# Top-32 attention on one core: the selection on quarters instead of halves of the scores

## The chip, the cores and the metric

The kernel runs on one core of a Trainium2 chip. The metric is the device time of one execution in microseconds (us). Three executions of the kernel before took 1880.09, 1892.16 and 1891.26 us; their median is 1891.26. A core has five engines that run at the same time, each through its own queue in order: TensorE (PE in the profile; PEld is its weight load), VectorE (DVE), ScalarE (ACT), GpSimd (POOL) and SyncE (SP, here for transfers). They wait for one another through semaphores.

## The reference

For each of 8 batches: 512 text rows `x` (256 wide) attend to 1024 context rows `cx` (192 wide) with 4 heads of 32. Of each row of 1024 scores only the 32 largest count; the softmax is over these. The mean over the heads weights the context; what comes out modulates a long convolution, an MLP and two layer norms, and then a mixture of 8 experts (one expert for each row, and a shared one).

```python
scores = einsum('bthd,bghd->bhtg', Q, K) / sqrt(DH)
topv, topi = top_k(scores, 32)
probs = softmax(topv, axis=-1)
attn = zeros_like(scores).at[bi, hi, ti, topi].set(probs)
attn_mean = attn.mean(axis=1)
...
x = x + tanh(g_xattn) * xattn(layernorm(x), ctx, ...)
x = x + tanh(g_ffn) * moe(layernorm(x), ...)
```

The masks are all true in these inputs.

## The kernel before

**Stages.** Batch by batch there are four streams of work: `prepare` (layer norm of `x`, keys `kT`, queries `qT`), `attention`, `mixed` with `after_mix` (convolution by a transform, modulation, MLP, shared expert), and `routed` (blocks of 128 rows for one expert each, whose results are added into `out` by indirect transfers that GpSimd issues). While batch b is in attention, batch b-1 is in `mixed` and `after_mix` (`behind`, L1378), batch b+1 in `prepare`, and the routed blocks of earlier batches lie between. After the last attention there is a tail of the last batch's `mixed`, `after_mix` and routed blocks.

**The order.** Nothing is issued directly. The class `Plan` (L50) notes every operation with an assumed duration (`time`, L137), its predecessors and its buffers. `order` (L220) then lays out all engines' queues by taking, among the operations that can begin first, the one noted earliest; `issue` (L318) issues them in that order. This is why nearly every instruction has line L326 in the profile. Where the plan finds TensorE idle, `busy` (L1407) puts in filler matmuls, `idle<-ones` at L1409, whose result nobody reads. A change of one operation therefore moves others on every engine.

**The attention step.** There are 64 steps: 8 batches, 4 tiles of 128 rows, 2 pairs of heads (L913). In each, for the two heads i of the pair:

- `scores` (L893), one step ahead: TensorE multiplies `qT` and `kT` into two PSUM banks, ScalarE copies these to `sc`, 128 rows by 1024 scores.
- The selection (L935 to L969). VectorE's `max` (MAX8 in the profile) returns the 8 largest of each row, `match_replace` overwrites these 8 so that the next `max` finds the next 8. Searching 1024 columns is avoided: score g and score g+512 form a pair. VectorE writes the higher of each pair to the first half of `mn` (L943), GpSimd the lower one to the second half, as integer sum less the higher one on the bits of the floats (L945, L946), so that no bit is lost. Four rounds of `max` and three of `match_replace` give the 32 largest of the 512 higher ones, with `left` as the working copy (L948 to L956); one `max` gives the 8 largest of the lower ones (L965). The 8th of the merged last eight and these eight is the 32nd largest score, `th` (L966 to L969), unless more than 8 of the 32 are lower ones.
- The weights. ScalarE computes exp into `e`; VectorE multiplies it by `score >= th` and sums it (L977, SCALAR_TENSOR_TENSOR); ScalarE counts by signs how many scores reach `th` (L979, `cnt`) and divides by the sum; GpSimd adds the heads into `acc` (L984). After both pairs `weighted` (L875) transposes `acc` and multiplies it with the context.

`mn`, `left`, `e`, `top` have two buffers each, `sc` four. At the end the kernel tests that every row had exactly 32 scores from `th` upward and that all masks are true (L1415 to L1424). If not, a general path computes everything again under `tc.If` (L1425).

Of the kernel before, what the change touches and what calls it, by code (L numbers as in the profile page):

```python
# [12 lines left out]
F32 = mybir.dt.float32  # L13
# [3 lines left out]
I32 = mybir.dt.int32  # L17
AF = mybir.ActivationFunctionType
ALU = mybir.AluOpType
# [3 lines left out]
P = 128  # L23
# [326 lines left out]
def tile_kernel(ctx: ExitStack, tc: tile.TileContext, a: dict, out: bass.AP):  # L350
# [3 lines left out]
    G, DV = cx.shape[1:]  # L354
    H, DH = 4, 32
    KTOP = 32
    HID = a["L0_xattn_W1"].shape[1]
    NST = a["L0_xattn_A_re"].shape[1]
    NE, _, NI = a["L0_ffn_rt_gate"].shape
# [4 lines left out]

    L = T // 2
    NL, NFFT = L // P, 2 * L
    SCALE = 1.0 / float(np.sqrt(np.float32(DH)))


# [15 lines left out]
    pk = ctx.enter_context(tc.tile_pool(name="pk", bufs=2))  # L385
# [10 lines left out]
    V, S, GP, TE, SY = (plan.engine(n, e) for n, e in (  # L396
        ("DVE", nc.vector), ("ACT", nc.scalar), ("POOL", nc.gpsimd), ("PE", nc.tensor), ("SP", nc.sync)))
# [495 lines left out]
    def scores(b, s, t, h0):  # L893

        plan.lead += LEAD_S
        n = f"{b}_{t}_{h0}"
        sc = [pq.tile([P, G], F32, tag="s", name=f"sc{n}_{i}") for i in range(2)]
        for q in range(G // 512):
            qs = slice(q * 512, (q + 1) * 512)
            pS = []  # L900
            for i in range(2):
                hp = slice((h0 + i) * DH, (h0 + i + 1) * DH)
                pS.append(ps_sc.tile([P, 512], F32, tag="sc", name=f"pS{n}_{i}_{q}", bufs=2))
                TE.matmul(pS[i], s.qT[hp, t * P : (t + 1) * P], s.kT[hp, qs], start=True, stop=True)
            for i in range(2):
                S.copy(sc[i][:, qs], pS[i])
        plan.lead -= LEAD_S
        return sc

    def attention(states):  # L910


        steps = [(b, t, h0) for b in range(B) for t in range(NT) for h0 in range(0, H, 2)]  # L913
        ahead = scores(0, states[0], 0, 0)
        behind = None
        for k, (b, t, h0) in enumerate(steps):
            s, sc = states[b], ahead
            if k + 1 < len(steps):
                b_, t_, h_ = steps[k + 1]
                for _ in states[b_].prep:  # L920
                    pass
                ahead = scores(b_, states[b_], t_, h_)
            if (t, h0) == (0, 0):


                s.uT = pk.tile([DK + 1, 2, T], F32, tag="uT", name=f"uT{b}")
                GP.memset(s.uT[DK : DK + 1, 0, :], 1.0)
            if h0 == 0:
                acc = pk.tile([P, G], F32, tag="acc", name=f"acc{b}_{t}")
            n = f"{b}_{t}_{h0}"  # L930

            top = pk.tile([P, 2, KTOP + 8], F32, tag="top", name="top" + n)  # L935
            sm = pk.tile([P, 5, 2], F32, tag="sm", name="sm" + n)
            nm, nb, na, su, ri = (sm[:, k_, :] for k_ in range(5))
            e_, mn = [], []
            for i in range(2):
                m_ = pk.tile([P, 2, G // 2], F32, tag="mn", name=f"mn{n}_{i}")  # L940
                mn.append(m_)
                lo, hi = sc[i][:, : G // 2], sc[i][:, G // 2 :]
                V.tensor_tensor(m_[:, 0], lo, hi, ALU.max)  # L943
                mi = m_.bitcast(I32)
                GP.tensor_tensor(mi[:, 1], lo.bitcast(I32), hi.bitcast(I32), ALU.add)  # L945
                GP.tensor_tensor(mi[:, 1], mi[:, 1], mi[:, 0], ALU.subtract)  # L946
            for i in range(2):
                for r in range(KTOP // 8):  # L948
                    t8 = top[:, i, r * 8 : r * 8 + 8]
                    src = mn[i][:, 0] if r == 0 else left  # L950
                    V.max(t8, src)
                    if r == 0:
                        S.activation(nm[:, i : i + 1], t8[:, 0:1], AF.Copy, scale=-SCALE)
                        left = pk.tile([P, G // 2], F32, tag="left", name=f"left{n}_{i}")
                    if r < KTOP // 8 - 1:
                        V.match_replace(left, t8, src, TAKEN)  # L956
                e_.append(pk.tile([P, G], F32, tag="e", name=f"e{n}_{i}"))
                S.activation(e_[i], sc[i], AF.Exp, bias=nm[:, i : i + 1], scale=SCALE)
                if i == 0:
                    yield  # L960
                    if behind is not None:
                        behind()
                        behind = None
            for i in range(2):
                V.max(top[:, i, KTOP:], mn[i][:, 1])  # L965
            t8 = pk.tile([P, 2, 8], F32, tag="t8", name="t8" + n)  # L966
            for i in range(2):
                V.max(t8[:, i, :], top[:, i, KTOP - 8 :])
            th = t8[:, :, 7]  # L969

            S.activation(na, th, AF.Abs, scale=EPS32)
            for i in range(2):
                S.activation(nb[:, i : i + 1], th[:, i : i + 1], AF.Identity, bias=na[:, i : i + 1],
                             scale=-1.0)
            for i in range(2):
                c = (b * NT + t) * H + h0 + i
                V.scalar_tensor_tensor(e_[i], sc[i], th[:, i : i + 1], e_[i], ALU.is_ge, ALU.mult,  # L977
                                       accum_out=su[:, i : i + 1])
                S.activation(junk, sc[i], AF.Sign, bias=nb[:, i : i + 1], accum_out=cnt[:, c : c + 1])  # L979
            V.reciprocal(ri, su)  # L980
            for i in range(2):
                S.activation(acc if h0 + i == 0 else e_[i], e_[i], AF.Copy, scale=ri[:, i : i + 1])
                if h0 + i:
                    GP.tensor_add(acc, acc, e_[i])  # L984
            if h0 + 2 == H:
                behind = partial(weighted, b, s, t, acc)
            yield
        behind()

    def attention_masked(b, s):  # L990
# [3 lines left out]
        for t in range(NT):  # L994
            acc = pk.tile([P, G], F32, tag="acc", name=f"acc{b}_{t}")
            for h in range(H):
# [14 lines left out]
                for r in range(KTOP // 8):  # L1011
                    src = sc if r == 0 else wk_
                    V.max(top[:, r * 8 : r * 8 + 8], src)
                    if r == 0:
                        GP.tensor_scalar(sm[:, 0:1], top[:, 0:1], -SCALE, None, ALU.mult)
                    V.match_replace(wk_, top[:, r * 8 : r * 8 + 8], src, TAKEN)

                S.activation(top, top, AF.Exp, bias=sm[:, 0:1], scale=SCALE, accum_out=sm[:, 1:2])
                S.activation(sc, sc, AF.Exp, bias=sm[:, 0:1], scale=SCALE)
                S.activation(wk_, wk_, AF.Exp, bias=sm[:, 0:1], scale=SCALE)  # L1020
                GP.tensor_sub(sc, sc, wk_)
# [353 lines left out]
    for _ in states[0].prep:  # L1375
        pass
    att = plan.ahead(attention(states), LEAD_A)
    def behind(b):  # L1378

        s_, between, n = mixed(b, states[b]), (), n_mix + n_mlp  # L1380
        rows = None
        if b - 1 in TAKE:
            k = TAKE[b - 1]
            if b == B - 1:
                rows = [rows_of(blk[b - 1], i, f"{b - 1}_{i}", "xb" if i < 2 else "left")
                        for i in range(k)]
            k0 = max(0, k - BETWEEN)
            if k0:
                s_ = beside((s_, n_mix), (routed(b - 1, 0, k0, rows), k0))
            between = routed(b - 1, k0, k, rows)  # L1390
            n += k
        return chain([s_, after_mix(b, states[b], between)]), n
# [96 lines left out]
```

## Time and profile before

| | |
|---|---|
| median of three executions | 1891.26 us |
| the profiled execution | 1877.53 us |
| its span, first to last instruction | 1875.8 us |
| TensorE's granted clock, mean | 0.955 |
| VectorE busy | 1465.7 us, 78% of the span |
| GpSimd busy | 1089.6 us, 58% |
| ScalarE busy | 1173.7 us, 63% |
| TensorE busy, 380.7 us of it fillers | 1712.8 us, 91% |
| first and last start of a write to `mn` | 34.5 and 1596.0 us |

The page's group rows read: line, engine, operation, output `<-` inputs by their names in the program, shapes, number of instructions; then busy time in us and mean duration in ns; then the idle time of that engine just before such instructions, and what ended it. The rows by tile give the least, the median and the greatest duration in ns. A window's row has its start and end, its length, and the busy time (and number of instructions) of each engine, then TensorE's clock and the share and rate of the transfers. An engine's busy time includes time in which an instruction has begun but is held up inside the engine. The profiled execution is one run; its time stands below the three others.

### The profile page before, as it was taken

The page shows a single profiled execution, that of the slowest core. Times are in us where ns is not written, and L with a number is a line of the kernel's source. Part 1 is how long each engine was busy: PE and PEld are TensorE (multiplying, and loading weights), DVE is VectorE, ACT ScalarE, POOL GpSimd, SP SyncE. Part 2 cuts the span into 40 slices and gives each one's busy share as a digit, 9 for nine tenths or more (in the row PEclk, how much of TensorE's full clock was granted, in tenths as well). Part 3 has the DMA queues.
Part 4 walks back from the last instruction along what each step waited for, and adds up shares of the span by engine and source line. Part 5 has one row for each costly group of instructions (what it writes and reads, how often), then busy time and mean ns, then how long its engine had stood idle before and what let it go on. Part 6 is the DMA issues. An engine that isn't in the chain of part 4 may idle for free. (4 is left out here: it accounts for less than half of the span.)

```text
span 1875.8 us, 24133 instructions
## 1 busy us (share of the span) xinstructions
PE 1712.8 (91%) x7888; PEld 992.7 (53%) x7888; DVE 1465.7 (78%) x2841; ACT 1173.7 (63%) x2020; POOL 1089.6 (58%) x1048
## 2 busy tenths in 40 slices
PE   8588997999989988999889889988999999999996
PEld 3254453445544554575447444654466546547685
DVE  4999988898889887989778989788998999531210
ACT  5577745577747764798469756976697678413221
POOL 5454435665765665577655856585758677532122
PEclk9799998999999988999989999998999999999998
DMA  4000010001100120044003320233013305532694
GB/s 113 0 1 23 20 46 17 1 12 57 57 17 12 56 62 17 23 132 127 17 12 115 94 79 12 71 111 107 12 49 104 118 1 148 170 118 76 188 289 127
DMA packets 101301, 131.88 MB, mean 70 GB/s; under 512 B 9687, under 2 KB 73004, under 8 KB 101166
## 3 DMA queue, kind: packets, MB, share of 16 engines
q1 hardware_dynamic: 93102, 121.05, 20.6%
q0 software_dynamic: 7008, 8.42, 2.6%
q8 instruction: 64, 1.05, 0.2%
q10 hardware_dynamic: 1056, 0.79, 0.1%
q14 instruction: 71, 0.58, 0.1%
HBM read 112.22 MB, written 18.78 MB: 70 GB/s over the span
## 5 line engine op out<-in xcount | busy, mean ns | idle before, releaser
L1409 PE MATMUL idle<-ones 128*128 128x512 bf16 x1525 | 380.7, 392 | 0.0
L326 POOL TENSOR_TENSOR acc<-acc,e 128x1024 f32<-128x1024 f32 x96 | 233.0, 2428 | 134.4 <-ACT e L326 131.9
L326 POOL TENSOR_TENSOR mn<-sc 128x512 int32<-128x512 int32 x128 | 204.0, 1603 | 155.3 <-DVE top L326 97.1
L326 DVE MAX8 top<-left 128x8 f32<-128x512 f32 x384 | 265.5, 691 | 10.4
L1409 PEld LDWEIGHTS <-ones 128*128 128x128 bf16 x1525 | 149.2, 101 | 197.6 <-issue 64.7
L326 DVE SCALAR_TENSOR_TENSOR e<-sc,t,e 128x1024 f32<-128x1024 f32 x128 | 210.3, 1660 | 18.2 <-ACT e L326 18.2
L326 PE MATMUL pS<-kT,qT 32*128 32x512 f32 x512 | 209.7, 663 | 13.9 <-ACT sc L326 13.4
L326 POOL TENSOR_TENSOR mn<-mn 128x512 int32<-128x512 int32 x128 | 180.8, 1424 | 64.7 <-DVE mn L326 61.4
L326 ACT COPY sc<-pS 128x512 f32<-128x512 f32 x256 | 142.8, 584 | 85.2 <-PE pS L326 65.9
L326 DVE MATCH_REPLACE8 left<-top,left 128x512 f32<-128x512 f32 x256 | 172.9, 675 | 0.0
L326 ACT ACT_TABLE_LOAD x130 | 166.8, 1283 | 7.8 <-PE p L326 2.1
L326 DVE MAX8 top<-mn 128x8 f32<-128x512 f32 x256 | 169.2, 679 | 3.0 <-POOL mn L326 2.7
L326 DVE TENSOR_TENSOR mn<-sc 128x512 f32<-128x512 f32 x128 | 150.1, 1198 | 24.8 <-ACT sc L326 24.8
L326 ACT ACTIVATE e<-sc,sm 128x1024 f32<-128x1024 f32 x128 | 146.1, 1148 | 30.7 <-POOL acc L326 27.2
L326 ACT ACTIVATE junk<-sc,sm 128x1024 bf16<-128x1024 f32 x128 | 146.3, 1143 | 1.3
L326 PE MATMUL pu<-aT,cx 128*96 128x128 f32 x1024 | 131.1, 277 | 0.9 <-ACT aT L326 0.9
L326 PEld LDWEIGHTS pu<-aT,cx 128*96 128x96 f32 x1024 | 119.5, 165 | 21.9 <-issue 15.2
L326 POOL DMA_INDIRECT out_dram<-yb,to x38 | 65.8, 1732 | 105.2 <-DMA out_dram<-yb,to 50.0
L326 PE MATMUL pm<-hT,w 128*128 128x512 f32 x256 | 119.1, 598 | 0.3
L326 PE MATMUL am<-w,ga 128*128 128x256 f32 x512 | 117.5, 380 | 2.0 <-ACT ga L326 2.0
L326 ACT ACTIVATE e<-e,sm 128x1024 f32<-128x1024 f32 x96 | 108.7, 1151 | 3.8 <-DVE sm L326 3.7
L326 PEld LDWEIGHTS pS<-kT,qT 32*128 32x128 f32 x512 | 57.7, 189 | 96.8 <-ACT sc L326 48.9
(288 smaller groups left out, 3165.8 us busy)
## 6 DMA issues: line engine op xcount, KB each, us to landing
rt_gate<-in_L_ffn_rt_gate_dram SPq DMA_DIRECT2D x38, 512.0 KB, 4.9
rt_up<-in_L_ffn_rt_up_dram SPq DMA_DIRECT2D x38, 512.0 KB, 3.7
rt_down<-in_L_ffn_rt_down_dram SPq DMA_DIRECT2D x38, 512.0 KB, 4.7
w<-in_L_xattn_W_dram SPq DMA_DIRECT2D x32, 512.0 KB, 4.1
cx<-in_ctx_dram SPq DMA_DIRECT2D x7, 768.0 KB
xtab<-zt SPq DMA_DIRECT2D x8, 642.5 KB, 4.1
xb<-xtab SPq DMA_DIRECT2D x38, 128.5 KB, 4.3
xt<-in_x_dram SPq DMA_DIRECT2D x8, 512.0 KB, 3.8
```

Source lines behind the costliest of these rows:

```text
L326: o.fn()
L1409: nc.tensor.matmul(idle, ones16, bc(ones16, 1, 4), start=True, stop=True)
```

## The change

Pairs become fours: scores g, g+256, g+512 and g+768 (`Q` is 256). For each head:

- VectorE writes the higher of g and g+512 to the first half of `mn`, as before, and then the higher of the two quarters of that half to a new tile `hi` (256 columns, in the buffers of the tag `left`).
- GpSimd writes the lower of each pair to the second half of `mn`, as before; two more instructions then replace the second quarter of `mn` with the lower of the two that `hi` compared. The last three quarters of `mn` (768 columns) then hold all scores that are not the highest of their four.
- The four rounds of `max` and three of `match_replace` run on 256 columns. The first one reads `hi`; the working copy `left` is no longer a tile of its own, but the first quarter of `mn`.
- One `max` of the remaining 768 columns gives their 8 largest.
- The GpSimd instructions are noted in a second loop, after both heads' first maximum.

```diff
+    Q = G // 4
...
-            e_, mn = [], []
+            e_, mn, hi = [], [], []
             for i in range(2):
-                m_ = pk.tile([P, 2, G // 2], F32, tag="mn", name=f"mn{n}_{i}")
+                m_ = pk.tile([P, G], F32, tag="mn", name=f"mn{n}_{i}")
                 mn.append(m_)
-                lo, hi = sc[i][:, : G // 2], sc[i][:, G // 2 :]
-                V.tensor_tensor(m_[:, 0], lo, hi, ALU.max)
-                mi = m_.bitcast(I32)
-                GP.tensor_tensor(mi[:, 1], lo.bitcast(I32), hi.bitcast(I32), ALU.add)
-                GP.tensor_tensor(mi[:, 1], mi[:, 1], mi[:, 0], ALU.subtract)
+                V.tensor_tensor(m_[:, : 2 * Q], sc[i][:, : 2 * Q], sc[i][:, 2 * Q :], ALU.max)
             for i in range(2):
+                m_ = mn[i]
+                hi.append(pk.tile([P, Q], F32, tag="left", name=f"hi{n}_{i}"))
+                V.tensor_tensor(hi[i], m_[:, :Q], m_[:, Q : 2 * Q], ALU.max)
+                mi, si = m_.bitcast(I32), sc[i].bitcast(I32)
+                GP.tensor_tensor(mi[:, 2 * Q :], si[:, : 2 * Q], si[:, 2 * Q :], ALU.add)
+                GP.tensor_tensor(mi[:, 2 * Q :], mi[:, 2 * Q :], mi[:, : 2 * Q], ALU.subtract)
+                GP.tensor_tensor(mi[:, Q : 2 * Q], mi[:, :Q], mi[:, Q : 2 * Q], ALU.add)
+                GP.tensor_tensor(mi[:, Q : 2 * Q], mi[:, Q : 2 * Q], hi[i].bitcast(I32), ALU.subtract)
+            for i in range(2):
+                left = mn[i][:, :Q]
                 for r in range(KTOP // 8):
                     t8 = top[:, i, r * 8 : r * 8 + 8]
-                    src = mn[i][:, 0] if r == 0 else left
+                    src = hi[i] if r == 0 else left
                     V.max(t8, src)
                     if r == 0:
                         S.activation(nm[:, i : i + 1], t8[:, 0:1], AF.Copy, scale=-SCALE)
-                        left = pk.tile([P, G // 2], F32, tag="left", name=f"left{n}_{i}")
                     if r < KTOP // 8 - 1:
                         V.match_replace(left, t8, src, TAKEN)
...
             for i in range(2):
-                V.max(top[:, i, KTOP:], mn[i][:, 1])
+                V.max(top[:, i, KTOP:], mn[i][:, Q:])
```

## The prediction

> **What bounds the kernel now.** I read the busy shares in 40 slices first.
>
> ```profile
> span 1875.8 us, 24133 instructions
> PE   8588997999989988999889889988999999999996
> DVE  4999988898889887989778989788998999531210
> POOL 5454435665765665577655856585758677532122
> ```
>
> The span has two parts. VectorE is at 7 to 9 tenths until about slice 34 and nearly idle after it. The first `mn` of the attention starts at 34.5 us and the last at 1596.0, so 64 steps take about 24.7 us each; the last 260 us hold no selection. The chain that ended last names only that tail (writes of `out_dram`), so it says nothing on the change. PE's row is misleading, as it contains fillers (L1409). The windows of the attention, all engines and then the fillers alone:
>
> ```profile
> 580.00:820.00 240.00, 224.41 (x886) 124.93 (x885) 207.63 (x415) 173.32 (x304) 150.21 (x150) 0.94 0.14 43
> 1060.00:1300.00 240.00, 216.64 (x910) 128.11 (x909) 204.54 (x390) 163.39 (x276) 155.62 (x146) 0.95 0.28 85
> 1300.00:1540.00 240.00, 231.75 (x954) 129.86 (x953) 221.01 (x439) 175.80 (x300) 168.47 (x160) 0.97 0.19 55
> 1300.00:1540.00 240.00, 29.47 (x115) 11.14 (x115) 0.97 0.19 55
> ```
>
> Columns: PE, PE's loads, VectorE, ScalarE, GpSimd. From 100 to 1540 us VectorE's six windows sum to 1269 of 1440 us, 88%; GpSimd's to 915, 64%. Without fillers PE has 186, 198 and 202 us of 240 in these windows, 78 to 84%. VectorE is the bound, with PE close behind. Then the groups and the durations by tile:
>
> ```profile
> L326 DVE MAX8 top<-left 128x8 f32<-128x512 f32 x384 | 265.5, 691 | 10.4
> L326 DVE MATCH_REPLACE8 left<-top,left 128x512 f32<-128x512 f32 x256 | 172.9, 675 | 0.0
> L326 DVE MAX8 top<-mn 128x8 f32<-128x512 f32 x256 | 169.2, 679 | 3.0 <-POOL mn L326 2.7
> ...
> L326 DVE MAX8 top<-mn x256: 660/676/696, 36.8 to 1607.6; 128x8 f32<-128x512 f32 x128
> L326 DVE TENSOR_TENSOR mn<-sc x128: 659/688/4997, 34.5 to 1590.5; 128x512 f32<-128x512 f32 x128
> L326 POOL TENSOR_TENSOR mn<-sc x128: 1253/1277/2264, 34.5 to 1596.0; 128x512 int32<-128x512 int32 x128
> ...
> 1047.45 2.36 POOL L326 TENSOR_TENSOR acc<-acc,e 128x1024 f32<-128x1024 f32 x1
> 1047.53 2.82 DVE L326 TENSOR_TENSOR mn<-sc 128x512 f32<-128x512 f32 x1
> ```
>
> MAX8 never varies; the maximum of two score halves does (659 to 4997 ns, mean 1198). The last two lines, from the order of time, show why: the VectorE maximum began 0.08 us after a GpSimd add and ended about 0.5 us after it, not in its own 0.69 us. VectorE waited on GpSimd for the selection only 2.7 us in all; both engines have slack toward each other today.
>
> [...] the trace has 732 ns (median, `xr<-xr,gout`) at 256 and 1277 at 512.
>
> **Part by part**, over 64 steps of two heads.
> - *MAX8.* Before 640 on 512 columns: 265.5+169.2 = 434.7 us. After 512 on 256 (217.1) and 128 on 768 (122.5)[...]: saves 95 us.
> - *Match-replace.* 384 go from 512 to 256 columns. [...] 259.4 becomes 156.7, saves 103 us. Their 384 value loads stay.
> - *The second maximum, `hi`.* 128 new instructions with two SBUF inputs. Unblocked as the 256-column tensor_tensor `xr<-xr,pfo`, 418 ns: adds 54 us. VectorE's own work falls by 95+103-54 = 144 us.
> - *GpSimd.* 256 more integer instructions on 256 columns, an estimate of 0.73 us each from the row above: 187 us, up to 0.87 each (223 us) if blocked like that row's mean. It lifts GpSimd from 64 to about 77% of the attention. Behind them in its queue stand the `acc` additions, the `yf` and `xr` additions, the layer-norm statistics and the 70 indirect transfers (65.8+35.1 us of issuing). Their number does not change; each can start about 3 us later, under the 36% of idle time that GpSimd has.
> - *Blocking.* Today the maxima lose 1198-690 = 0.51 us each and the e products 1660-1270 = 0.39: 65+50 = 115 us. With 21% more GpSimd work they lose 24 us more. Each `hi` follows straight on the maximum whose end also starts GpSimd's subtraction. No trace shows this; bounds are 0 and one subtraction, 1.28 us. I take the maxima's 0.5: 64 us.
> - *The new wait.* `left` is now written over the quarter-maxima in `mn`, which GpSimd must have read: the first match-replace of each head waits for GpSimd's third instruction, and all VectorE work stands behind it, the e products and PE's `xm`, `ge` and `ger` among it. In the changed kernel's instruction order I summed by row durations, for each head, what GpSimd has from the 512-column subtraction to that instruction, and what VectorE has from its maximum to the match-replace. In 24 of 128 heads GpSimd's part is longer, by 48 us in all (bounds: 0, and 128 times subtraction and add, 256 us). In 20 of 64 steps only the two short MAX8 stand between the last `hi` and the wait, so cover is thin.
> - These two losses share time, since a blocked `hi` lets GpSimd advance. Half of the shorter as shared: 64+48-24 = 88 us.
> - *At nothing:* ScalarE's `nm` and exp get their input a little earlier, ScalarE being 70% busy; buffers keep their number, and only 1.5 us in the trace wait for `left`; SP and its transfers are untouched; 37 of 1525 fillers go, in PE's idle time. The tail has no selection.
>
> Sum: 144-24-88 = 32 us off VectorE, of which 88% (its share of the stretch) reach the end: 28 us. The profiled execution took 1877.5 us (span 1875.8), 0.73% under the median of 1891.3; 1849.5 scaled to the median is **1863 us**.
>
> **The cases.**
> 1. *VectorE stays the bound, most of the gain is lost to blocking* (45%): 1863, own range 1840 to 1890 by `hi` at 0.25 to 0.75 us and the wait at 20 to 70 us.
> 2. *The losses hide* (17%): the waits find other VectorE work and `hi` loses 0.15 us. 144-24-20 = 100, times 0.88 = 88 us: about 1803. For it: 104 of 128 heads have cover enough by the durations. Against it: those durations take no account of blocking.
> 3. [...] (24%, slower). [...] The addition is 240 us in all against 144 saved: it turns slower where over 60% of it is exposed (case 1: 112 of 240, 47%). At 75% it is 180-144 = +36: about 1927. Against it: GpSimd's idle time, 520 us in the attention.
> 4. *No change* (14%): VectorE is freed, but PE at 84% and its chains through `pfi`, `pu`, `py` (VectorE waited 54 us for `pfi`, and 91 for the routed blocks' `pu`, part of it in the tail) set the step: within 1% of 1891.
> That the selection fails and the general path runs is a rival too: it would double the time. By the reference's inputs, of 16,384 rows of scores one has 7 of its 32 largest outside the highest of their fours, none has over 7, and 8 are allowed; under 1%, inside case 3.
>
> **Numbers.** The shown runs differ by 0.6%, so 1% is about what a measurement can tell from no change. Case 1 is split 30 faster, 15 same: faster 0.30+0.17 = 0.47, same 0.15+0.14 = 0.29, slower 0.24. The range 1805 to 1925 leaves out half of case 2 and half of case 3.
>
> **What would show it.** MAX8 at about 0.42 and 0.96 us, match-replace near 0.41; `hi` near 0.9 with a minimum of 0.42; GpSimd near 77%; VectorE waiting on POOL `mn` before match-replace for some 20 to 70 us, 2.7 before. VectorE's share below 80% with a step still near 24.7 us would speak for case 3 or 4: for 3 if maxima and products grow well over 1.2 and 1.7 us, for 4 if PE without fillers rises. If `hi` stays near 0.5 us and the step falls under 23.5, case 2 holds.

## The result, and the profile after

| | before | after |
|---|---|---|
| median of the executions | 1885.92 us (4) | 1913.62 us (4) |
| ratio after to before, 95% interval | | 1.0149 (1.0116 to 1.0183) |
| the profiled execution, its span | 1877.53, 1875.8 us | 1912.57, 1910.8 us |
| VectorE busy | 1465.7 us | 1411.0 us |
| GpSimd busy | 1089.6 us | 1305.8 us |

The change makes the kernel 1.5% slower; 1.5% faster was predicted as the likeliest. The busy shares of the page of after, and its windows of the attention (columns as before: PE, PE's loads, VectorE, ScalarE, GpSimd):

```profile
span 1910.8 us, 24502 instructions
DVE  5999989697859787888996879777977998531210
POOL 6566547686957687788886969696968887632122
```

```profile
580.00:820.00 240.00, 225.12 (x846) 116.55 (x844) 195.87 (x440) 171.72 (x299) 187.64 (x193) 0.96 0.11 33
1060.00:1300.00 240.00, 225.54 (x886) 126.49 (x885) 194.19 (x422) 163.52 (x282) 195.09 (x206) 0.94 0.26 76
1300.00:1540.00 240.00, 227.69 (x942) 129.84 (x938) 200.47 (x426) 164.72 (x283) 192.00 (x185) 0.96 0.23 66
```

GpSimd is busy for 188 to 195 of 240 us, where it was at 150 to 168; over 100 to 1540 us it went from 915 to 1088 us, 76%. VectorE fell from 1269 to 1191 us there, 83%. Both engines now have holes: neither is full, and the attention still takes longer (first to last maximum on `sc` 32.8 to 1615.4 us, before 34.5 to 1590.5). The tail is as long as it was: 268 us from the start of the last MAX8 on `mn` before, 270 after. The groups of the selection, each shape apart (busy us, mean ns, idle time before):

```profile
L326 DVE MAX8 top<-mn 128x8 f32<-128x256 f32 x384 | 163.6, 426 | 11.9
L326 DVE TENSOR_TENSOR mn<-sc 128x512 f32<-128x512 f32 x128 | 148.1, 1179 | 32.9 <-ACT sc L326 32.9
L326 DVE TENSOR_TENSOR hi<-mn 128x256 f32<-128x256 f32 x128 | 138.8, 1111 | 1.0
L326 DVE MAX8 top<-mn 128x8 f32<-128x768 f32 x128 | 118.9, 944 | 9.0 <-POOL mn L326 8.9
L326 POOL TENSOR_TENSOR mn<-mn 128x256 int32<-128x256 int32 x128 | 112.2, 876 | 11.4 <-DVE hi L326 7.3
L326 POOL TENSOR_TENSOR mn<-mn,hi 128x256 int32<-128x256 int32 x128 | 109.8, 858 | 8.6
L326 DVE MATCH_REPLACE8 mn<-top,mn 128x256 f32<-128x256 f32 x256 | 104.5, 408 | 0.0
L326 DVE MATCH_REPLACE8 mn<-top,hi 128x256 f32<-128x256 f32 x128 | 52.2, 408 | 0.0
L326 DVE MAX8 top<-hi 128x8 f32<-128x256 f32 x128 | 49.8, 412 | 0.5
```

The narrow searches cost about what was reckoned. `hi` doesn't: 1111 ns for an instruction that takes 391 at its shortest (least, median and greatest in the first line), and VectorE's waits on GpSimd's `mn` went from 2.7 to 54 us: 45 before the first match-replace, 9 before the last MAX8 (the next two lines, from the list of waits: total, times, longest):

```profile
L326 DVE TENSOR_TENSOR hi<-mn x128: 391/1272/3015, 35.1 to 1618.9; 128x256 f32<-128x256 f32 x128
```

```profile
DVE mn L326 <- POOL mn L326: 45.4, 28, 5.4
DVE top L326 <- POOL mn L326: 8.9, 6, 2.0
```

In the two profiled executions the span grew by 35 us: VectorE was busy for 55 us less and idle for 90 more. Of these 90, 52 are the waits on `mn`; three other waits make up the other 38, on TensorE's `am` and `pfi` and on ScalarE's `sc` (of before, then of after):

```profile
DVE xm L326 <- PE pfi L326: 54.5, 20, 8.7
DVE xr L326 <- PE am L326: 34.1, 2, 33.6
DVE mn L326 <- ACT sc L326: 24.8, 10, 5.5
...
DVE xm L326 <- PE pfi L326: 64.3, 21, 11.4
DVE xr L326 <- PE am L326: 54.4, 6, 33.6
DVE mn L326 <- ACT sc L326: 32.9, 20, 3.3
```

Two stretches in order of time (start, length, instruction, in brackets the idle time before it and what ended it) show both losses. First a blocked `hi`, then the longest wait:

```profile
1206.52 1.73 POOL L326 TENSOR_TENSOR mn<-sc 128x512 int32<-128x512 int32 x1
1207.16 1.38 DVE L326 TENSOR_TENSOR hi<-mn 128x256 f32<-128x256 f32 x1
...
561.90 2.36 POOL L326 TENSOR_TENSOR acc<-acc,e 128x1024 f32<-128x1024 f32 x1
...
564.22 5.21 POOL L326 TENSOR_TENSOR yf<-yf,t 128x512 f32<-128x512 f32 x5
...
569.39 0.72 POOL L326 TENSOR_TENSOR mn<-mn 128x256 int32<-128x256 int32 x1
570.14 0.09 DVE L326 MATCH_VALUE_LOAD mn<-top,hi 128x8 f32 x1 [5.40 <-POOL mn L326]
```

`hi` begins inside a GpSimd addition and ends 0.29 us after it. In the second stretch VectorE stands 5.4 us before a match-replace because GpSimd's third instruction of that head is queued behind an `acc` addition and five of `yf`.

### The profile page after: what moved, and what is told of

Its sections match the earlier page's. It is cut to its first block, busy times and chain, and to the rows that moved or that the text cites. A ratio compares the mean times of both kernels' runs of the same rounds, so it can differ in the third digit from the quotient of the medians.

```text
span 1910.8 us, 24502 instructions
## 1 busy us (share of the span) xinstructions
PE 1754.0 (92%) x7851; PEld 1006.0 (53%) x7851; DVE 1411.0 (74%) x2969; ACT 1167.8 (61%) x2016; POOL 1305.8 (68%) x1304
## 5 line engine op out<-in xcount | busy, mean ns | idle before, releaser
L326 POOL TENSOR_TENSOR mn<-mn 128x512 int32<-128x512 int32 (+1 forms) x256 | 291.2, 1141 | 61.2 <-DVE mn L326 46.2
L326 DVE MAX8 top<-mn 128x8 f32<-128x256 f32 (+1 forms) x512 | 276.8, 555 | 20.9 <-POOL mn L326 8.9
L326 PE MATMUL pS<-kT,qT 32*128 32x512 f32 x512 | 243.5, 698 | 23.2 <-ACT sc L326 22.6
L326 POOL TENSOR_TENSOR mn<-sc 128x512 int32<-128x512 int32 x128 | 195.2, 1530 | 100.4 <-DVE top L326 44.6
L326 DVE SCALAR_TENSOR_TENSOR e<-sc,t,e 128x1024 f32<-128x1024 f32 x128 | 208.9, 1642 | 20.1 <-ACT e L326 19.1
L326 DVE TENSOR_TENSOR mn<-sc 128x512 f32<-128x512 f32 x128 | 148.1, 1179 | 32.9 <-ACT sc L326 32.9
L326 DVE TENSOR_TENSOR hi<-mn 128x256 f32<-128x256 f32 x128 | 138.8, 1111 | 1.0
L326 PEld LDWEIGHTS pS<-kT,qT 32*128 32x128 f32 x512 | 65.8, 197 | 116.5 <-ACT sc L326 53.4
L326 POOL TENSOR_TENSOR mn<-mn,hi 128x256 int32<-128x256 int32 x128 | 109.8, 858 | 8.6
L326 POOL TENSOR_TENSOR yf<-yf,t 128x512 f32<-128x512 f32 (+1 forms) x80 | 94.3, 1202 | 25.5 <-DVE t L326 24.2
```

The costliest lines, as they stand in the source:

```text
L326: o.fn()
```

## The experiments

Times are medians of runs beside runs of the kernel before on the same chip; "before" there is 1884 to 1888 us.

| kernel | median us | less the kernel before | ratio, 95% interval |
|---|---|---|---|
| a_own_left | 1881.6 | -2.8 | 0.9997 (0.9977 to 1.0018) |
| a_hi_reduce | 1890.4 | +6.0 | 1.0034 (1.0010 to 1.0057) |
| b_pool_load | 1902.2 | +17.8 | 1.0110 (1.0050 to 1.0170) |
| a_low_dve | 1970.0 | +85.6 | 1.0435 (1.0376 to 1.0494) |
| a_own_left_hi_reduce | 1861.4 | -22.7 | 0.9864 (0.9820 to 0.9908) |
| a_more_fill | 1913.7 | +29.6 | 1.0155 (1.0120 to 1.0191) |
| b_more_fill | 1895.1 | +11.1 | 1.0057 (1.0032 to 1.0082) |
| a_low_dve_more_fill | 1960.3 | +76.2 | 1.0394 (1.0352 to 1.0436) |
| c_no_low | 1837.2 | -47.5 | 0.9740 (0.9701 to 0.9779) |
| a_plan_hi | 1921.2 | +36.5 | 1.0204 (1.0160 to 1.0247) |
| a_low_dve_plan | 1950.5 | +65.8 | 1.0340 (1.0300 to 1.0380) |
| a_all_reduce | 1843.1 | -41.6 | 0.9775 (0.9731 to 0.9819) |
| b_mn_reduce | 1864.2 | -23.7 | 0.9896 (0.9819 to 0.9973) |
| a_low_reduce | 1885.9 | -2.0 | 1.0015 (0.9983 to 1.0046) |

Names with a start from the changed kernel, those with b from the one before; c leaves out part of the computation. The theories: W, the new wait before the match-replace costs the time; P, GpSimd's added work does, by itself and in that it and VectorE's two-input instructions hold each other up; H, TensorE's clock; R, an order laid out for wrong durations.

### The new wait, the blocked maximum, GpSimd's load

**a_own_left** takes the cause of the new wait away:

```diff
-                hi.append(pk.tile([P, Q], F32, tag="left", name=f"hi{n}_{i}"))
+                hi.append(pk.tile([P, Q], F32, tag="hi", name=f"hi{n}_{i}"))
...
-                left = mn[i][:, :Q]
+                left = pk.tile([P, Q], F32, tag="left", name=f"left{n}_{i}")
```

> The changed kernel with `left` as a tile of its own again, so that the first match-replace overwrites nothing that GpSimd has still to read; all instructions and sizes stay. Theory W (the new wait costs the time): VectorE's 45 us of waiting on POOL `mn` before match-replace go, and the time falls by 35 to 50 us, to 1865-1880. Theory P [...]: `hi` stays near 1.1 us, the wait moves to the last MAX8 of each head, which needs GpSimd's fourth instruction, and the time stays within 15 us of 1913.

It came to 1881.6 us, 32 less than the changed kernel. Theory W has nearly the size it claimed. No wait before a match-replace is left in its list of waits; at the last MAX8, which needs GpSimd's fourth instruction, it grew to this:

```profile
DVE top L326 <- POOL mn L326: 30.1, 22, 3.3
```

So 54 us of waiting became 30. VectorE's busy time also fell, by 20 us: `hi` from 1111 to 940 ns, the maxima on `sc` from 1179 to 1068. The planner lays out a new order without the dependency, so the 32 us are those of the wait and of the order together. Theory P isn't refuted by that: `hi` still took 940 ns.

**a_hi_reduce** makes `hi` with one SBUF input:

```diff
-                V.tensor_tensor(hi[i], m_[:, :Q], m_[:, Q : 2 * Q], ALU.max)
+                V.tensor_reduce(hi[i], m_[:, : 2 * Q].rearrange("p (k q) -> p q k", k=2), AX.X, ALU.max)
```

> The changed kernel with `hi` made by a reduction over a view of `mn` (one SBUF input of 512 elements) instead of a maximum of two SBUF inputs of 256. Theory P: the reduction takes a steady 0.69 us where the maximum took 1.11 on average and 0.39 at least, VectorE's `hi` falls from 139 to about 88 us, GpSimd is held up less, and the time falls by 30 to 50 us, to 1865-1885. Theory W: what `hi` gains is waited for at the match-replace, whose wait grows from 45 to 70 us or more, and the time stays within 15 us of 1913.

The planner takes both forms as equally long (0.68 us), and all 7851 matmuls of the two traces stand in the same order; only this one instruction differs. By tile:

```profile
L326 DVE TENSOR_REDUCE hi<-mn x128: 659/686/704, 35.4 to 1603.1; 128x256 f32<-128x512 f32 x128
```

Twice the elements, and the time is steady: 0.69 us where the maximum ranged from 0.39 to 3.0. Its spread is 45 ns, beside a GpSimd that is busy for 1089 of the 1440 us from 100 to 1540, as it was in the changed kernel (1088). VectorE's busy time fell by 56 us (1411.0 to 1354.8), its wait before match-replace rose from 45 to 57, and the time fell by 23 us: between the two theories, short of the 30 us that P asked for at least.

```profile
DVE mn L326 <- POOL mn L326: 56.6, 36, 5.4
```

**b_pool_load** adds the load to the kernel before:

```diff
                 GP.tensor_tensor(mi[:, 1], mi[:, 1], mi[:, 0], ALU.subtract)
+                lq, uq = mi[:, 1, : G // 4], mi[:, 0, : G // 4]
+                GP.tensor_tensor(lq, lq, uq, ALU.add)
+                GP.tensor_tensor(lq, lq, uq, ALU.subtract)
```

> The kernel before with two more GpSimd instructions for each head, an integer add and a subtract on 256 columns that leave the lower halves as they were; VectorE's work is unchanged and only the MAX8 of the lower ones waits for them. Theory P: GpSimd's busy time grows by 200 to 220 us, maxima and products of two SBUF inputs grow by 0.1 to 0.2 us each, and the time rises by 30 to 60 us, to 1915-1945. Theory W: GpSimd has 36% idle time, the waits have cover, and the time stays within 12 us of the kernel before.

18 us slower, less than theory P claimed and more than W allowed. Its line of busy times, against 1465.7 us of VectorE and 1089.6 of GpSimd before:

```profile
PE 1732.3 (92%) x7893; PEld 998.6 (53%) x7893; DVE 1485.5 (78%) x2841; ACT 1177.5 (62%) x2023; POOL 1287.5 (68%) x1304
```

GpSimd's busy time rose by 198 us; VectorE's only by 20, of which the products took 8 and the maxima 2. GpSimd's load costs. How much of it comes from longer blocking and how much from GpSimd's later results, this run doesn't tell.

**a_low_dve** gives the second lower ones to VectorE:

```diff
-                GP.tensor_tensor(mi[:, Q : 2 * Q], mi[:, :Q], mi[:, Q : 2 * Q], ALU.add)
-                GP.tensor_tensor(mi[:, Q : 2 * Q], mi[:, Q : 2 * Q], hi[i].bitcast(I32), ALU.subtract)
+                low.append(pk.tile([P, Q], F32, tag="low", name=f"low{n}_{i}"))
+                V.tensor_tensor(low[i], m_[:, :Q], m_[:, Q : 2 * Q], ALU.min)
...
-                left = mn[i][:, :Q]
+                left = hi[i]
...
-                V.max(top[:, i, KTOP:], mn[i][:, Q:])
+                V.max(top[:, i, KTOP : KTOP + 8], mn[i][:, 2 * Q :])
+                V.max(top[:, i, KTOP + 8 :], low[i])
```

> The changed kernel with the lower ones of the second step made by VectorE (a minimum of two SBUF inputs on 256 columns into a tile of their own, and a MAX8 on 512 and one on 256 columns in place of the one on 768), and `left` in place of `hi`; GpSimd's two added instructions are gone, and with them the new wait. VectorE gets 128 minima (0.4 to 1.1 us each) and 0.15 us more of MAX8 for each head: 70 to 160 us more work, which would take back most of its saving. Theory P: GpSimd's load is as before, and the time is that of the kernel before or a little more, 1880-1905. Theory W: the same 45 us of waiting go but VectorE's work counts in full: 1915-1960.

Both theories missed: 1970 us, with VectorE only 25 us busier than before (1490.9) and GpSimd back at 1084. `hi` took 1041 ns, `low` 966. a_low_reduce, further on, shows what made it slow.

### Both edits together, and a theory on TensorE's clock

The traces record TensorE's granted clock as either full or half. In a_low_dve it was half for 327 us, in the changed kernel for 225, in the kernel before for 172. That gave a third theory, H: unforeseen gaps on TensorE cost its clock. The edit is one number:

```diff
-FILL_MAX, FILL, STEP = 12.0, 0.85, 0.22
+FILL_MAX, FILL, STEP = 12.0, 1.0, 0.22
```

> The changed kernel with the share of planned idle time that fillers cover raised from 0.85 to 1.0 (1797 fillers for 1488). Theory H: VectorE's waits on GpSimd make gaps on TensorE that the plan does not foresee, TensorE falls to half clock for 225 us in place of 172, and that is a good part of the loss; more fillers bring the half-clock time under 190 us and the time down by 10 to 25 us. Theories W and P: TensorE isn't the bound, the time stays within 8 us of 1913 or rises by what the fillers hold up.

> The kernel before with the same raised share (1851 fillers for 1525), to see what the fillers do without the change. Theory H: it has fewer unforeseen gaps, so it gains less than the changed kernel does, 0 to 10 us. Theories W and P: within 8 us of before.

> The kernel a_low_dve (1970 us, half clock for 327 us, granted clock 0.918) with the same raised share. Theory H: its 85 us over the kernel before are mostly TensorE at half clock (155 us more of it, some 78 us of lost work), and the fillers bring it down by 30 us or more. Without theory H it stays within 12 us of 1970.

(The traces have 1752 and 1792 fillers, not 1797 and 1851.) The half-clock time fell to 170, 148 and 250 us, by 55, 24 and 77. The time did not follow: 1913.7 us against 1913.6, 11 us slower in the kernel before, 10 faster in a_low_dve. So more fillers don't give back the loss, and theory H missed its forecast. It isn't refuted either, since fillers occupy TensorE themselves (44 to 53 us more in the three traces). An estimate from these three pairs: fillers that cost some 20 us each time, and half-clock time that costs 0.4 us for each us, would give the same 0, +11 and -10; the 53 us more of half clock in the changed kernel would then stand for some 20 us. No run here takes the two apart. In the kernels with one of the two losses removed the half-clock time is shorter too (201 us in a_own_left, 212 in a_hi_reduce), so the clock may be one of the ways in which these losses cost time.

**a_own_left_hi_reduce** has the first two edits.

> The changed kernel with both earlier edits: `left` as a tile of its own and `hi` by a reduction with one SBUF input. Alone they gave 32 and 23 us. If the new wait and the blocked `hi` are two separate losses (theories W and P together), the time is about 1913-32-23 = 1858 us, 1.4% under the kernel before. If they are one loss (VectorE waits for GpSimd in one place or the other), it stays at 1875-1890.

1861.4 us, where the sum of both gave 1858. The gains add up: they are two losses, not one seen in two places.

### The load again, the order, and the selection without two-input maxima

**c_no_low** leaves out GpSimd's two added instructions, on top of both edits; the last line keeps the final test from starting the general path:

```diff
-                GP.tensor_tensor(mi[:, Q : 2 * Q], mi[:, :Q], mi[:, Q : 2 * Q], ALU.add)
-                GP.tensor_tensor(mi[:, Q : 2 * Q], mi[:, Q : 2 * Q], hi[i].bitcast(I32), ALU.subtract)
...
-    V.tensor_scalar(cnt, cnt, float(2 * KTOP - G), None, ALU.is_equal)
+    V.tensor_scalar(cnt, cnt, -1e9, None, ALU.is_ge)
```

> a_own_left_hi_reduce (1861 us) without GpSimd's two added instructions for each head. It leaves out part of the computation: the second quarter of `mn` keeps the higher ones of the pairs, so that the 8 largest of the rest, the threshold and the weights are not the reference's; the final test of the counts is set to hold always, so that the general path stays out of it. VectorE's instructions and sizes are the same. Theory P's other half (GpSimd's added work costs time by itself, as the 18 us in b_pool_load): 15 to 30 us less, 1832-1847. If that load is covered once the wait and the blocked `hi` are gone: within 8 us of 1861.

1837.2 us, 24 less. With the 18 of b_pool_load that is the price of GpSimd's added work, from two sides. Two things fell with it in the traces: VectorE, with the same instructions, was busy for 35 us less (1363.1 to 1328.4), and its wait for GpSimd before the last MAX8 went from 24.2 us to 4.8. This kernel is also the narrow selection without the three losses (the wait, the blocked `hi`, the load), and it shows what the narrow search is worth. The page's lines of busy times, of the kernel before, of a_own_left_hi_reduce and of c_no_low:

```profile
PE 1712.8 (91%) x7888; PEld 992.7 (53%) x7888; DVE 1465.7 (78%) x2841; ACT 1173.7 (63%) x2020; POOL 1089.6 (58%) x1048
```

```profile
PE 1709.2 (92%) x7749; PEld 991.9 (53%) x7749; DVE 1363.1 (73%) x2969; ACT 1165.1 (63%) x2012; POOL 1294.4 (70%) x1304
```

```profile
PE 1690.0 (92%) x7718; PEld 981.8 (53%) x7718; DVE 1328.4 (72%) x2969; ACT 1163.9 (63%) x2014; POOL 1101.1 (60%) x1048
```

Against the kernel before, VectorE has 137 us less to do and the kernel gains 47: about a third. The list of its waits shows where some of the rest went, where the kernel before had 54.5 and 34.1 us (total, times, longest):

```profile
DVE xm L326 <- PE pfi L326: 85.7, 24, 13.3
...
DVE xr L326 <- PE am L326: 58.2, 7, 33.6
```

**a_plan_hi** and **a_low_dve_plan** change only the planner's assumption:

```diff
             op.cost, op.table = self.time(eng, method, out, outs, ins, args, kw, n)
+            if eng == "DVE" and method == "tensor_tensor" and op.what[1].startswith(("hi", "low")):
+                op.cost = 1.1
```

> The changed kernel with the same instructions, in which the planner's assumed duration of a `hi` maximum is the measured 1.1 us in place of 0.68; only the order of the queues moves. Theory R (the planner lays out an order for durations that don't hold, and the queues wait for it): the time falls by 15 to 30 us. Theories W and P: the wait and the blocking stay where they are, within 10 us of 1913.

> a_low_dve (1970 us) with the planner's assumed duration of the `hi` maximum and the `low` minimum at 1.1 us in place of 0.68, near their measured 1.04 and 0.97. Theory R: its surprising 85 us over the kernel before, with VectorE's busy time only 25 us higher, are an order that doesn't fit; the time falls by 40 us or more. Without theory R: within 12 us of 1970.

The changed kernel became 8 us slower with the better estimate, a_low_dve 20 us faster (intervals of 7 and 15 us either way). The wrong price for `hi` is not what made the change slow. Other orders stay untried. A new order alone moved these two kernels by 8 and 20 us, so every difference between runs with different orders may hold some of that.

**a_all_reduce** makes the first maximum with one SBUF input as well, on top of both edits:

```diff
-                V.tensor_tensor(m_[:, : 2 * Q], sc[i][:, : 2 * Q], sc[i][:, 2 * Q :], ALU.max)
+                V.tensor_reduce(m_[:, : 2 * Q], sc[i].rearrange("p (k q) -> p q k", k=2), AX.X, ALU.max)
```

> a_own_left_hi_reduce with the first maximum of the selection as a reduction too (one SBUF input of 1024 elements for two of 512): about 1.22 us for a mean of 1.05 with blocking and 0.69 without. VectorE's work rises by 22 us, but no selection instruction has two SBUF inputs any more. Theory P [...]: GpSimd is held up less and the time falls below 1861, by 5 to 20 us. If VectorE's own time decides: it rises by 5 to 15 us.

1843.1 us, 18 less than a_own_left_hi_reduce, though VectorE's busy time rose by 9 us. GpSimd's fell by 45, from 1294.4, with the same 1304 instructions on record (the page's line of busy times):

```profile
PE 1694.0 (92%) x7771; PEld 988.1 (54%) x7771; DVE 1372.5 (75%) x2969; ACT 1161.1 (63%) x2012; POOL 1249.2 (68%) x1304
```

The reduction itself, by tile, is as steady as the one for `hi`:

```profile
L326 DVE TENSOR_REDUCE mn<-sc x128: 1208/1230/1272, 32.6 to 1546.6; 128x512 f32<-128x1024 f32 x128
```

So what was gained here was not VectorE's time; GpSimd's shorter work is what the trace shows, but the queues have a new order as well, and the run doesn't part the two. This kernel beats both: 2.2% under the one before.

### What stayed open after these

**b_mn_reduce** is the same edit in the kernel before, **a_low_reduce** is a_low_dve with both of its 256-column instructions as reductions:

```diff
-                V.tensor_tensor(m_[:, 0], lo, hi, ALU.max)
+                V.tensor_reduce(m_[:, 0], sc[i].rearrange("p (k q) -> p q k", k=2), AX.X, ALU.max)
```

> The kernel before with the maximum of the score halves as a reduction with one SBUF input of 1024 elements. Theory P: VectorE's time for it stays near 1.2 us (1.20 with blocking before), GpSimd is held up less, and the time falls by 5 to 20 us from the kernel before, about as it did in a_all_reduce (18 us). [...]

> a_low_dve (1970 us) with `hi` and `low` as reductions with one SBUF input of 512 elements, 0.69 us each for 1.04 and 0.97. Theory P: VectorE's work falls by 80 us, [...] and the time falls by 40 to 80 us, to 1890-1930. If the slowness of a_low_dve lies elsewhere (its 128 additional instructions, `left` in place of `hi`): above 1945.

b_mn_reduce gained 24 us with no other change of the selection: VectorE 8 us busier, GpSimd 33 us less. This is the same sign as in a_all_reduce, in another kernel and another order, so the kernel before already paid for its two-input maxima; the interval, 5 to 34 us, is wide.

```profile
PE 1725.2 (92%) x7912; PEld 1000.3 (54%) x7912; DVE 1473.3 (79%) x2841; ACT 1166.8 (63%) x2016; POOL 1056.3 (57%) x1048
```

a_low_reduce came to 1885.9, 84 us under a_low_dve, for 86 us less of VectorE's busy time (1490.9 to 1404.7); theory P is right here, and a little beyond its own range. As both forms have nearly the same price in the planner, the order hardly moves (7765 of some 7807 matmuls stand in the same order). The slowness of a_low_dve was its four two-input instructions of 256 columns in each step. The line of busy times of a_low_reduce:

```profile
PE 1729.7 (92%) x7807; PEld 998.0 (53%) x7807; DVE 1404.7 (74%) x3225; ACT 1168.1 (62%) x2016; POOL 1068.7 (57%) x1048
```

## Why the prediction was wrong

Put in a row, the runs split the result. Each step is a difference of medians, with an interval of 4 to 9 us either way. The steps run from one kernel to the next, so that their sum meets the result by construction and tests nothing. In each the planner lays out the queues anew; where the order stayed the same, in a_hi_reduce, `hi` was worth 23 us.

| from, to | us | what it is |
|---|---|---|
| before to c_no_low | -47 | the narrow search without the three losses below |
| c_no_low to a_own_left_hi_reduce | +24 | GpSimd's 256 added instructions |
| to a_own_left | +20 | `hi` with two SBUF inputs |
| to the changed kernel | +32 | `left` in place, the new wait, with its order |
| sum | +29 | measured +28 (1913.6 less 1885.9) |

Step by step:
- *MAX8 and match-replace* came out as reckoned. 434.7 us became 332.3, 102 saved for 95 (213.4 us for 217.1 on 256 columns, 118.9 for 122.5 on 768); match-replace took 156.7, as in the sum. The durations at the new widths were the author's estimates, not shown by the trace of before; the trace of after has MAX8 at 426 and 412 ns on 256 columns and at 944 on 768, match-replace at 408.
- *`hi`*: 54 plus 64 us were reckoned, 138.8 measured. Blocking was 0.7 us each and not 0.5; the term was mis-sized by 21 us.
- *The older two-input instructions* were to lose 24 us more; the products and maxima lost none (208.9 for 210.3 and 148.1 for 150.1 us). VectorE's other, smaller instructions, which had no term, took some 15 us more.
- *The new wait*: 48 us from the queues, 45 in the trace before the match-replace. Right in mechanism and size. Another 6 us of waiting at the last MAX8 (8.9 for 2.7) had no term.
- *"Half of the shorter as shared"* failed. With an unblocked `hi` the wait grew from 45 to 57 us (a_hi_reduce), but a_own_left_hi_reduce shows the two gains in time as additive. On VectorE 205 us were saved by the searches and 3 in the older instructions; 139 for `hi` and 15 in the smaller instructions leave 55 less of busy time, and 52 more of waiting leave some 3 us off VectorE, against the 32 predicted.
- *"GpSimd from 64 to about 77%", each instruction behind it starting 3 us later under its idle time*: the share was right (76%), the price of nothing was wrong. It is the first term that failed: 18 to 24 us by b_pool_load and c_no_low, though GpSimd had 36% of idle time. How these divide between blocking on VectorE and results that came later is not shown.
- *"88% (its share of the stretch) reach the end"* is the second, and the larger: c_no_low kept 47 of 137 us, about a third. Share of busy time was taken for the rate at which savings come through; but VectorE's own waits on TensorE grew as it became faster (by 55 us at `pfi` and `am` in c_no_low). That is a part of case 4, which was given as a case of its own and not as a factor on case 1. With 0.34 (47 of 137) of the 144 us unblocked, the gain is 49; the blocking, the wait and the load, measured at 20 to 32 each, together outweigh it. That puts measured steps into the prediction's sum, and so it shows which terms failed, but tests nothing new.
- *Case 3*, in which GpSimd and VectorE's two-input instructions bound each other, had the sign and nearly the time (1927). That its time came so near is luck. Its 240 us take in the 54 of `hi`, which had been taken off the 144 saved already; without them 75% of 187 is 140, and the case comes out at no change. Its own sign, maxima and products well over 1.2 and 1.7 us, didn't show either: 1.18 and 1.64. That two-input instructions beside GpSimd cost time is shown: by a_hi_reduce (23 us) and a_low_reduce (84), and, in new orders, by a_all_reduce (18) and b_mn_reduce (24). What joins the two engines, no run shows. The biggest single loss was the new wait (32 us with its order), which that case didn't price. That the general path did not run, as foreseen, shows in the time.
- The planner's price for `hi` was tried and is not the cause. Whether part of the loss comes by way of TensorE's clock stays open.

With the two-input maxima taken out of the selection on both sides, a_all_reduce stands 18 us under b_mn_reduce, each against the kernel before on its own chip: the idea of quarters gains about 1% there, but with intervals that touch (0.9731 to 0.9819, 0.9819 to 0.9973). What stays open is how the 90 us that VectorE saved in c_no_low and that did not reach the end divide among TensorE, ScalarE and the new order; the waits show 55 of them at `pfi` and `am`, and no run took these apart.

## What to carry to other kernels

A busy share of 88% does not mean that 88% of a saving arrives. Here 47 of 137 us of VectorE's busy time came through in c_no_low and 23 of 56 in a_hi_reduce, but 84 of 86 in a_low_reduce: where other engines stand near 80% in the same stretch, price the saving with a wide range, and ask which wait of the bound engine will grow in its place. When work goes to an engine with slack, look at who waits behind it in its queue, and see that the new place of a buffer does not make the bound engine wait for it. VectorE instructions with two SBUF inputs beside a busy GpSimd were dear here (`hi` took 1111 ns on average, 391 at least); a reduction over a strided view of one input does the same maximum (0.69 us, steadily).

## What the runs showed of the hardware

The reduction over pairs 256 or 512 elements apart took 0.69 us for 512 input elements and 1.23 us for 1024, with a spread of 45 to 64 ns beside a busy GpSimd (a_hi_reduce, a_all_reduce); a maximum of two inputs took 0.39 to 3.0 us at 256 columns (the changed kernel). With 128 maxima of 512 columns made by reductions, GpSimd was busy for 33 and 45 us less, about 0.3 us for each (b_mn_reduce, a_all_reduce, both in a new order). TensorE's half-clock time fell by 55 us with more fillers, without any gain in time (a_more_fill).
